# A graph-attention stack: the adjacency mask built beside the first batch, and one clock for all batches

## The chip, the cores and the metric

The kernel runs on one core of a Trainium2 chip. The metric is the device time of one execution in microseconds (us). The core has a matrix engine (TensorE; in profiles PE, its weight loads PEld), VectorE (DVE), ScalarE (ACT), GpSimd (POOL) and a queue for transfers (SP). Each engine takes its instructions from a queue of its own, and semaphores tie the queues together.

## The reference, cut to what matters

x has 32 batches of 512 nodes with 256 features; adj is one 512 x 512 matrix of integers, the same for all batches. Four layers run one after the other on each batch, each with a residual connection:

```python
h = jnp.maximum(_layernorm(x, axis=-1), 0.0)
x = x + layer(h)        # layers 0, 1, 2, 3

# inside a layer, graph attention
Wh = h @ W
e = leaky_relu((Wh @ a1)[:, :, None] + (Wh @ a2)[:, None, :])
e = where(mask, e, -inf)
out = softmax(e) @ Wh
```

Layer 0 uses the mask (adj > 0) or the diagonal. Layer 1 has another slope, layer 2 has four heads, and layer 3 has a linear layer, an attention over all nodes with no mask and 512 features, a second linear layer and a masked attention. Batches don't depend on one another.

## The kernel before, in words

The kernel has a fast path, `fast`, and a general path that runs only when a flag says that the fast path's assumptions about the data don't hold. All times here are those of the fast path.

**Arithmetic.** Exponentials of the two halves of the logit are taken per node, so that one weight of the attention is a maximum times the mask: `weights` (L335) turns a column with four transposes and makes four tiles of 128 x 512 by `max` and a product with `maskT` on VectorE (L343). `maskT` is the mask, transposed, in bfloat16; every masked layer of every batch reads it. `values` (L300) multiplies the turned activations by W and scales the result. `aggregate` (L353) multiplies weights by values. W has three more columns, products of W with the attention vectors; `finish_w` (L131) makes them with `project` (L107): transposes, a copy on ScalarE, small matmuls, and a copy on VectorE (L120). In layer 3, `sort_attend` (L527) replaces the unmasked attention by a sort: nodes are ranked by comparison scans on VectorE, scattered to DRAM in order by GpSimd's indirect transfers (L571), summed up in prefix and suffix sums (L588 to L612), and gathered back (L619). The very last batch uses `attend` (L495), which does this attention as dense matmuls.

**Order.** Four streams (`NS = 4`) take every fourth batch each. A batch is a Python generator that yields, after each piece of work, the time at which its next piece is due on a clock of the kernel's own. The loop at L722 always continues the stream with the earliest due time. A due time is made in `after_us` (L62) from what the piece spends on TensorE by a count (`spent`) and from a latency in us; a stream's own factor, `pace`, stretches both:

```python
def after_us(us):
    return begun[0] + pace[turn[0]] * (STRETCH * spent[0] / CYCLES + SLOW * us)
```

Streams start 75 clock-us apart (`LEAD`). `pace` is 1 until a stream reaches its last batch; then L713 sets it to 1.15 for batch 28, 1.025 for batch 29, 0.9 for batch 30 and 0.775 for batch 31. The clock is only a means to write instructions in an order: nothing waits for it on the chip. A fifth generator, `setup` (L213), prepares what later layers need (W1, W2, WFC, WHA, triangles for the sort); it is due at 0 and then every 4 clock-us, and draws its PSUM banks from stream 3. `bank` (L74) gives each stream two of the eight PSUM banks, by `turn`.

The order in which the program is written is a priority. The framework's scheduler builds each engine's queue from it with its own estimate of when operands are there, and may put an instruction that it thinks ready early ahead of others: in the trace, the memset of L232, written in the middle of `setup`, runs at 1.54 us. `tc.keep_in_program_order` pins an instruction behind everything that was written for its engine before it, without a wait.

**The start.** Ahead of all streams the program loads x of four batches, W0 and adj, finishes W0, and makes the mask (L190 to L202): `own` is adj > 0 on VectorE (L191), GpSimd puts ones on the diagonal (L192), sixteen transposes on TensorE and four copies on ScalarE make `maskT`. In `setup`, a reduction of adj to its least element (L218) feeds the flag.

Of the kernel before, what the change touches and what calls it, by code (L numbers as in the profile page):

```python
# [19 lines left out]
FP = mybir.dt.float32  # L20
# [4 lines left out]
OP = mybir.AluOpType  # L25
AX = mybir.AxisListType

EPS = 1.0e-5
P = 128
# [3 lines left out]
CYCLES = 2400.0  # L33
# [3 lines left out]
def fast(ctx, tc, flag, x, adj, w0, a0, w1, a1, w2, a2, mlp1_w, mlp1_b, mlp2_w, mlp2_b,  # L37
         w_fc, a_fc, w_hand, a_hand, out):
    nc = tc.nc
    B, N, F = x.shape  # L40
    NT = N // P
# [5 lines left out]
    NS = 4  # L47
    LEAD = 75.0
    SLOW = 1.5
    STRETCH = 2.0  # L50

    const = ctx.enter_context(tc.tile_pool(name="const", bufs=1))
    work = ctx.enter_context(tc.tile_pool(name="work", bufs=2))
# [3 lines left out]
    turn = [0]  # L57
    begun = [0.0]
    spent = [0.0]
    pace = [1.0] * NS  # L60

    def after_us(us):  # L62

        return begun[0] + pace[turn[0]] * (STRETCH * spent[0] / CYCLES + SLOW * us)

    def matmul(p, w, x, **flags):
        spent[0] += 4 * max(x.shape[-1], P)
        nc.tensor.matmul(p, w, x, **flags)  # L68

    def transpose(p, x, i):  # L70
        spent[0] += 2 * P
        nc.tensor.transpose(p, x, i)  # L72

    def bank():  # L74
        return psum.tile([P, N], FP, tag=f"b{turn[0]}", name="b", bufs=8 // NS)
# [3 lines left out]
    ident = const.tile([P, P], FP, name="ident")  # L79
# [23 lines left out]
    def scale_a(t, alpha):  # L103
        nc.vector.tensor_scalar_mul(t[:, :, 1:2], t[:, :, 0:1], alpha - 1.0)
        nc.vector.tensor_scalar_mul(t[:, :, 2:3], t[:, :, 2:3], 1.0 - alpha)

    def project(dst, block, k, a_cols):  # L107

        ft, n = a_cols.shape[1], a_cols.shape[2]
        p = bank()  # L110
        for f in range(ft):
            transpose(p[:, f * P:(f + 1) * P], block(k, f), ident)
        wT = work.tile([P, N], FP, tag="y", name="wT", bufs=3)
        nc.scalar.copy(wT[:, :ft * P], p[:, :ft * P])
        q = bank()
        for f in range(ft):
            matmul(
                q[:, :n], wT[:, f * P:(f + 1) * P], a_cols[:, f, :], start=(f == 0), stop=(f == ft - 1)
            )
        nc.vector.tensor_copy(dst, q[:, :n] if len(dst.shape) == 2 else q[:, :n].rearrange("p (h c) -> p h c", c=3))  # L120
# [10 lines left out]
    def finish_w(fetched, alpha):  # L131
        t, a_cols = fetched

        def block(k, f):
            c = f * P + (3 if f * P >= F else 0)
            return t[:, k, c:c + P]

        scale_a(a_cols, alpha)
        for k in range(t.shape[1]):
            project(t[:, k, F:F + 3], block, k, a_cols)  # L140
            yield
# [4 lines left out]
    adj_sb = work.tile([P, NT, N], I32, tag="w", name="adj", bufs=4)  # L146
# [10 lines left out]
    for h in range(NH):  # L157
        t, r = divmod(h * D, P)
# [27 lines left out]
    for _ in finish_w(fetched0, 0.2):  # L186
        pass


    own = work.tile([P, NT, N], FP, tag="w", name="own", bufs=4)  # L190
    nc.vector.tensor_scalar(own, adj_sb, 0.0, None, op0=OP.is_gt)  # L191
    nc.gpsimd.affine_select(  # L192
        out=own, in_=own, pattern=[[P, NT], [-1, N]], base=0, channel_multiplier=1,
        compare_op=OP.not_equal, fill=1.0,
    )
    maskT = const.tile([P, NT, N], BF, name="maskT")
    for j in range(NT):
        turn[0] = j % NS
        p = bank()
        for t in range(NT):  # L200
            transpose(p[:, t * P:(t + 1) * P], own[:, t, j * P:(j + 1) * P], ident)
        nc.scalar.copy(maskT[:, j, :], p)  # L202

    before = const.tile([P, P], FP, name="before")
    after = const.tile([P, P], FP, name="after")
    band = const.tile([P, 2 * N - P], BF, name="band")
    differ = const.tile([P, 2], FP, name="differ")
# [4 lines left out]

    def setup():  # L213

        yield from finish_w(fetched1, 0.01)


        nc.vector.tensor_reduce(differ[:, 0:1], adj_sb, AX.XY, OP.min)  # L218
        nc.vector.tensor_scalar(differ[:, 0:1], differ[:, 0:1], 0.0, None, op0=OP.is_lt)
        least = small([1], "rden")  # L220
        nc.vector.tensor_reduce(least, diag, AX.X, OP.min)
        nc.vector.tensor_scalar(differ[:, 1:2], least, 0.0, None, op0=OP.is_le)
        nc.vector.tensor_copy(W2[:, :, :, :D], raw2.rearrange("p k (h d) -> p k h d", d=D))
        nc.vector.tensor_scalar_mul(A2v[:, :, 1:2], A2v[:, :, 0:1], -0.8)
        nc.vector.tensor_scalar_mul(A2v[:, :, 2:3], A2v[:, :, 2:3], 0.8)
        for k in range(KF):
            project(W2[:, k, :, D:], lambda k, f: raw2[:, k, f * P:(f + 1) * P], k, A2)
            yield
        yield from finish_w(fetched3, 0.2)

        for tri, sign in ((before, 1), (after, -1)):
            nc.vector.memset(tri, 1.0)  # L232
            nc.gpsimd.affine_select(
                out=tri, in_=tri, pattern=[[sign, P]], base=0, channel_multiplier=-sign,
                compare_op=OP.is_gt, fill=0.0,
            )
        ties = work.tile([P, 2 * N - P], FP, tag="w", name="ties", bufs=4)
        nc.vector.memset(ties, TINY)
        nc.gpsimd.affine_select(
            out=ties, in_=ties, pattern=[[-1, 2 * N - P]], base=N - P, channel_multiplier=1,  # L240
            compare_op=OP.is_gt, fill=0.0,
        )
        nc.vector.tensor_copy(band, ties)
        yield
        yield from finish_w(fetched4, 0.2)
# [3 lines left out]
    def small(shape, name):  # L249
        return work.tile([P] + shape, FP, tag=name, name=name, bufs=2 * NS)  # L250
# [25 lines left out]
    def turn_pair(xn, hT, t0):  # L276
        p = bank()
        for k in range(KF):
            for i in range(2):
                c = (k * 2 + i) * P  # L280
                transpose(p[:, c:c + P], xn[:, t0 + i, k * P:(k + 1) * P], ident)
        nc.scalar.activation(hT[:, :, t0 * P:(t0 + 2) * P], p.rearrange("p (k n) -> p k n", k=KF), AF.Relu)  # L282

    def turned(xn, when):

        hT = work.tile([P, KF, N], FP, tag="hT", name="hT", bufs=3)
        turn_pair(xn, hT, 0)
        yield when
        turn_pair(xn, hT, 2)
        yield after_us(0.6)  # L290
        return hT
# [8 lines left out]
    def values(hT, w, rs=None):  # L300

        v = work.tile([P, NT, F + 3], FP, tag="v", name="v", bufs=4)
        for t in range(NT):
            ps = bank()
            for k in range(KF):
                matmul(
                    ps[:, :F + 3], hT[:, k, t * P:(t + 1) * P], w[:, k, :], start=(k == 0), stop=(k == KF - 1)
                )
            pj = v[:, t, F:F + 1]
            if rs is None:  # L310
                nc.scalar.activation(v[:, t, F:], ps[:, F:F + 3], AF.Exp)  # L311
                nc.scalar.activation(v[:, t, :F], ps[:, :F], AF.Copy, scale=pj)
            else:
                nc.scalar.activation(v[:, t, F:], ps[:, F:F + 3], AF.Exp, scale=rs[:, t:t + 1])
                nc.vector.tensor_scalar(  # L315
                    v[:, t, :F], ps[:, :F], rs[:, t:t + 1], pj, op0=OP.mult, op1=OP.mult
                )
            if t + 1 < NT:
                yield after_us(0)
        yield after_us(0.8)  # L320
        return v
# [372 lines left out]
    def batch(b):  # L694
        xt = xts.pop(b)
        xn, rs = new_xn(), small([NT], "rs")
        for t0 in range(0, NT, 2):
            norm(xt, xn, rs, t0, False)
        yield after_us(4)
        when = after_us(2)  # L700
        for layer in (layer0, layer1, layer2):
            xn, rs, when = yield from layer(xt, xn, rs, when)
        if b + NS < B:
            xts[b + NS] = load_x(b + NS)
        yield from layer3(xt, xn, when, b)
# [2 lines left out]

    def stream(first):
        for b in range(first, B, NS):  # L710

            if b >= B - NS:
                pace[first] = 1.15 - (NS - B + b) / (2 * NS)  # L713
            yield from batch(b)

    ready = {i: i * LEAD for i in range(NS)}
    streams = [stream(i) for i in range(NS)]
    early = setup()  # L720
    ready[NS] = 0.0
    while ready:  # L722
        i = min(ready, key=ready.get)
        if i == NS:
# [20 lines left out]
    p = bank()  # L745
# [401 lines left out]
@with_exitstack  # L1147
def kernel(ctx: ExitStack, tc: tile.TileContext, *args):
    nc = tc.nc
    keep = ctx.enter_context(tc.tile_pool(name="keep", bufs=1))  # L1150
    flag = keep.tile([1, 1], I32, name="flag")
    fast(tc, flag, *args)
    bad = nc.values_load(flag[0:1, 0:1], min_val=0, max_val=1)
    with tc.If(bad > 0):
        general(tc, *args)
# [27 lines left out]
```

## Time and profile before

| | |
|---|---|
| time, median of 3 runs | 3026.18 us (3023.26 to 3026.87) |
| span of the profiled execution | 3030.3 us |
| VectorE busy | 2269.9 us, 75% |
| ScalarE busy | 1489.6 us, 49% |
| GpSimd busy | 470.2 us, 16% |
| transfers | 245.46 MB, mean 81 GB/s |

In the page, "busy" is the time in which an engine executes; a group's line has the source line, the engine, the operation, what it writes and reads, and how often. Most matmuls are recorded by one helper, so they carry line L68, and all transposes line L72; there the names of the tiles tell what is what (`b<-W,hT` is `values`, `b<-v,w` an aggregate, `b<-ident,xn` the turning of a batch's normalised input). A matmul on float32 appears as two instructions. The timeline view lists start, duration, engine, line and tiles, and in brackets how long the engine stood idle before and what ended that.

### The profile page before, as it was taken

How to read it: one execution, taken by the hardware profiler on the slowest of the kernel's cores; microseconds unless marked ns; L12 is line 12 of the kernel's file. 1: busy time of each engine (PE TensorE's matmuls, PEld its weight loads, DVE VectorE, ACT ScalarE, POOL GpSimd, SP SyncE). 2: the span in 40 equal slices, each digit the busy share in tenths (PEclk: the TensorE clock that was granted, in tenths of full speed). 3: DMA queues.
4: the chain of work that ended last, by engine and by line, in shares of the span. 5: the costliest groups of instructions: out<-in, count | busy, mean ns of one | idle time of the engine just before them, and what ended most of it. 6: DMA issues, size and time to landing. Idle time of an engine off the chain costs nothing. (4 is left out here: it accounts for less than half of the span.)

```text
span 3030.3 us, 43501 instructions
## 1 busy us (share of the span) xinstructions
PE 2924.8 (97%) x15529; PEld 2368.3 (78%) x15529; DVE 2269.9 (75%) x5674; ACT 1489.6 (49%) x3758; POOL 470.2 (16%) x509
## 2 busy tenths in 40 slices
PE   7999999999999999999999999999999999999897
PEld 5787887877788877788877788877888877788665
DVE  4588778777877777777778777877877877767664
ACT  3444455554455554455554455554455554454445
POOL 0011111101111201112111111101111111111111
PEclk8999999999999999999999999999999999999999
DMA  3022223222223222223232223222223222212220
GB/s 91 1 88 87 75 74 102 83 90 88 74 74 102 84 89 83 80 74 102 78 95 82 81 74 102 83 90 91 71 74 102 89 84 87 74 52 82 84 97 29
DMA packets 178685, 245.46 MB, mean 81 GB/s; under 512 B 15328, under 2 KB 153886, under 8 KB 178464
## 3 DMA queue, kind: packets, MB, share of 16 engines
q1 hardware_dynamic: 148704, 144.32, 14.9%
q0 software_dynamic: 29760, 98.30, 9.8%
q8 instruction: 125, 2.05, 0.3%
q14 instruction: 96, 0.79, 0.1%
HBM read 127.46 MB, written 115.12 MB: 80 GB/s over the span
## 5 line engine op out<-in xcount | busy, mean ns | idle before, releaser
L68 PE MATMUL b<-v,w 128*128 128x257 f32 (+1 forms) x7232 | 1225.5, 322 | 22.0 <-DVE w L343 8.6
L68 PEld LDWEIGHTS b<-v,w 128*128 128x128 f32 x7232 | 1054.2, 192 | 186.7 <-issue 51.7
L343 DVE SCALAR_TENSOR_TENSOR w<-b,v,maskT 128x512 f32<-128x512 f32 x896 | 635.7, 743 | 13.3 <-PE b L72 10.5
L68 PE MATMUL b<-WFC,oT 128*128 128x256 f32 (+1 forms) x2048 | 491.5, 380 | 0.8 <-ACT v L311 0.5
L68 PEld LDWEIGHTS b<-WFC,oT 128*128 128x128 f32 x2048 | 373.6, 189 | 50.8 <-issue 1.0
L68 PE MATMUL b<-W,hT 128*128 128x259 f32 (+1 forms) x1536 | 389.1, 391 | 9.8 <-DVE v L315 8.6
L68 PEld LDWEIGHTS b<-W,hT 128*128 128x128 f32 x1536 | 282.8, 192 | 60.2 <-DVE v L315 11.0
L571 POOL DMA_INDIRECT order<-v,at x248 | 251.1, 1013 | 462.7 <-DVE seen L298 139.9
L68 PE MATMUL b<-hT,WM 128*128 128x512 f32 x512 | 251.9, 598 | 8.2 <-ACT hT L282 7.8
L359 DVE RECIPROCAL rden<-b 128x1 f32<-128x1 f32 (+1 forms) x516 | 80.2, 163 | 233.6 <-PE b L68 230.6
L677 POOL TENSOR_TENSOR x<-x,y 128x512 f32<-128x512 f32 x64 | 81.2, 1269 | 1077.3 <-ACT y L675 980.8
L619 POOL DMA_INDIRECT g<-table,at x124 | 122.5, 988 | 790.8 <-ACT y L639 287.1
L68 PE MATMUL b<-oT,WM 128*128 128x512 f32 x512 | 232.8, 597 | 0.0
L261 DVE BATCH_NORM_STATS2 st<-x 128x6 f32<-128x256 f32 x512 | 193.2, 409 | 5.6 <-DMA x<-in_x_dram 2.7
L331 ACT ACTIVATE oT<-b,bias 128x512 f32<-128x512 f32 x128 | 87.5, 686 | 216.6 <-PE b L68 216.4
L384 DVE TENSOR_TENSOR y<-q,y 128x512 f32<-128x512 f32 x192 | 132.5, 691 | 67.1 <-ACT q L383 48.2
L72 PEld LDWEIGHTS b<-ident,xn 128*128 128x128 f32 x1024 | 125.9, 142 | 69.9 <-DVE xn L272 23.6
L493 ACT ACTIVATE v<-b,ends 128x256 f32<-128x256 f32 x256 | 120.3, 470 | 122.2 <-PE b L68 115.6
L72 PE MATMUL b<-ident,xn 128*128 128x128 f32 x1024 | 159.7, 278 | 20.4 <-DVE xn L272 8.7
L282 ACT ACTIVATE hT<-b 128x512 f32<-128x512 f32 x256 | 150.2, 593 | 40.7 <-PE b L72 39.6
L68 PEld LDWEIGHTS b<-oT,WM 128*128 128x128 f32 x512 | 95.3, 191 | 93.5 <-issue 91.4
L638 ACT ACTIVATE q<-g,rden 128x512 f32<-128x512 f32 x124 | 89.5, 722 | 145.9 <-DVE rden L359 142.7
(139 smaller groups left out, 3735.0 us busy)
## 6 DMA issues: line engine op xcount, KB each, us to landing
table<-sums SPq DMA_DIRECT2D x62, 1032.0 KB
sums<-order SPq DMA_DIRECT2D x62, 516.0 KB
x<-in_x_dram SPq DMA_DIRECT2D x32, 512.0 KB
out_dram<-x SPq DMA_DIRECT2D x64, 256.0 KB
sums<-order SPq DMA_DIRECT2D x62, 129.0 KB
order<-v,at POOLq DMA_INDIRECT x248, 2.5
g<-table,at POOLq DMA_INDIRECT x124, 4.5
adj<-in_adj_dram SPq DMA_DIRECT2D x1, 1024.0 KB
```

What stands on the lines that cost most here:

```text
L68: nc.tensor.matmul(p, w, x, **flags)
L72: nc.tensor.transpose(p, x, i)
L261: nc.vector.bn_stats(st[:, i, :], xt[:, t0 + i, :])
L282: nc.scalar.activation(hT[:, :, t0 * P:(t0 + 2) * P], p.rearrange("p (k n) -> p k n", k=KF), AF.Relu)
L331: nc.scalar.activation(o[:, f, :], p, AF.Relu, bias=bias[:, f:f + 1])
L343: nc.vector.scalar_tensor_tensor(wt[:, j, :], r, t_col(j), maskT[:, j, :], op0=OP.max, op1=OP.mult)
L384: nc.vector.tensor_tensor(r, q, r, op=OP.add)
L493: nc.scalar.activation(halves[c][:, t, :F], ps[:, :F], AF.Copy, scale=ends[:, t, 0:1])
L571: nc.gpsimd.indirect_dma_start(out=orders[c], out_offset=bass.IndirectOffsetOnAxis(ap=at[:, 0, t:t + 1], axis=0), in_=halves[c][:, t, :], ...
L619: nc.gpsimd.indirect_dma_start(out=g, out_offset=None, in_=table, in_offset=bass.IndirectOffsetOnAxis(ap=at[:, 1, t:t + 1], axis=0),)
L638: nc.scalar.activation(q, z, AF.Exp, scale=rd)
L677: nc.gpsimd.tensor_tensor(xr, xr, y, op=OP.add)
```

## The change

Two things change. The mask moves from ahead of the streams into the first step of `setup`, which is now due at 7.5 on the kernel's clock, after the first pieces of batch 0; its banks come from streams 3, 2 and 1, so that those of stream 0 stay free. Its first transpose is pinned in TensorE's queue, and the reduction of adj in VectorE's. This is for letting batch 0 start beside the mask. And `pace` goes: the last four batches run on the same clock as all others.

```diff
-    pace = [1.0] * NS
 
     def after_us(us):
 
-        return begun[0] + pace[turn[0]] * (STRETCH * spent[0] / CYCLES + SLOW * us)
+        return begun[0] + STRETCH * spent[0] / CYCLES + SLOW * us
...
-    def transpose(p, x, i):
+    def transpose(p, x, i, tied=False):
         spent[0] += 2 * P
-        nc.tensor.transpose(p, x, i)
+        instruction = nc.tensor.transpose(p, x, i)
+        if tied:
+            tc.keep_in_program_order(instruction)
...
-    own = work.tile([P, NT, N], FP, tag="w", name="own", bufs=4)
-    nc.vector.tensor_scalar(own, adj_sb, 0.0, None, op0=OP.is_gt)
-    nc.gpsimd.affine_select(
-        out=own, in_=own, pattern=[[P, NT], [-1, N]], base=0, channel_multiplier=1,
-        compare_op=OP.not_equal, fill=1.0,
-    )
     maskT = const.tile([P, NT, N], BF, name="maskT")
-    for j in range(NT):
-        turn[0] = j % NS
-        p = bank()
-        for t in range(NT):
-            transpose(p[:, t * P:(t + 1) * P], own[:, t, j * P:(j + 1) * P], ident)
-        nc.scalar.copy(maskT[:, j, :], p)
-
...
     def setup():
 
+        own = work.tile([P, NT, N], FP, tag="w", name="own", bufs=4)
+        nc.vector.tensor_scalar(own, adj_sb, 0.0, None, op0=OP.is_gt)
+        nc.gpsimd.affine_select(
+            out=own, in_=own, pattern=[[P, NT], [-1, N]], base=0, channel_multiplier=1,
+            compare_op=OP.not_equal, fill=1.0,
+        )
+        for j in range(NT):
+            turn[0] = NS - 1 - j % (NS - 1)
+            p = bank()
+            for t in range(NT):
+                transpose(p[:, t * P:(t + 1) * P], own[:, t, j * P:(j + 1) * P], ident, j + t == 0)
+            nc.scalar.copy(maskT[:, j, :], p)
+        turn[0] = NS - 1
+        yield
         yield from finish_w(fetched1, 0.01)
 
 
-        nc.vector.tensor_reduce(differ[:, 0:1], adj_sb, AX.XY, OP.min)
+        tc.keep_in_program_order(nc.vector.tensor_reduce(differ[:, 0:1], adj_sb, AX.XY, OP.min))
...
     def stream(first):
         for b in range(first, B, NS):
-
-            if b >= B - NS:
-                pace[first] = 1.15 - (NS - B + b) / (2 * NS)
             yield from batch(b)
...
-    ready[NS] = 0.0
+    ready[NS] = 7.5
```

## The prediction

> **What bounds the kernel now.** I read the page's busy table first, then the span in stretches of 300 us, then the timeline of the first 25 us, and at the end the same windows view cut at the places where batches end, the waits of TensorE there, and GpSimd's timeline for those ends.
>
> ```profile
> PE 2924.8 (97%) x15529; PEld 2368.3 (78%) x15529; DVE 2269.9 (75%) x5674; ACT 1489.6 (49%) x3758; POOL 470.2 (16%) x509
> ```
>
> TensorE is busy 97% of the span: only its idle time, and the time at a low clock, can be won. Where is the idle time? The windows view has the stretch, then busy us of PE, PEld, DVE, ACT, POOL, and the granted clock:
>
> ```profile
> 0.00:300.00 300.00, 272.20 (x1438) 220.97 (x1439) 199.48 (x541) 122.48 (x323) 29.17 (x38) 0.96 0.21 66
> 1200.00:1500.00 300.00, 295.39 (x1603) 242.71 (x1601) 232.50 (x580) 157.38 (x403) 48.54 (x54) 1.00 0.27 87
> 2700.00:3031.00 331.00, 294.51 (x1436) 225.83 (x1434) 200.62 (x474) 151.03 (x353) 51.19 (x53) 0.96 0.21 69
> ```
>
> The middle loses 4.6 us in 300 (1.5%), the first 300 us lose 27.8 and the last 331 lose 36.5. The change touches just these two ends. Timeline of the start:
>
> ```profile
> 10.08 1.23 DVE L191 TENSOR_SCALAR own<-adj 128x2048 f32<-128x2048 int32 x1 [2.22 <-DMA adj<-in_adj_dram]
> 11.22 0.15 DVE L120 COPY W<-b 128x3 f32<-128x3 f32 x1
> 11.29 2.28 DVE L218 TENSOR_REDUCE differ<-adj 128x1 f32<-128x2048 int32 x1
> 11.38 1.92 POOL L192 TENSOR_SCALAR_AFFINE_SELECT own<-own 128x2048 f32<-128x2048 f32 x1 [9.06 <-DVE W L120]
> 13.35 3.54 PE L72 MATMUL b<-ident,own 128*128 128x128 f32 x16 [3.11 <-POOL own L192]
> 13.49 0.15 DVE L120 COPY W<-b 128x3 f32<-128x3 f32 x1
> 16.72 0.71 PE L72 MATMUL b<-ident,xn 128*128 128x128 f32 x5
> 18.06 1.14 PE L68 MATMUL b<-W,hT 128*128 128x259 f32 x4
> 23.69 0.75 DVE L343 SCALAR_TENSOR_TENSOR w<-b,v,maskT 128x512 f32<-128x512 f32 x1 [0.22 <-PE b L72]
> ```
>
> TensorE stands 3.11 us before the mask's transposes, and batch 0, whose xn has been ready since 7.86 (the last of the three L272 rows: 6.81 + 1.05), queues behind them to 16.6. W0's last three columns come at 13.64, behind the 2.28 us reduction of adj.
>
> At the end, GpSimd's last additions (two per batch) show when batches 27 to 31 end: 2759, 2929, 2979, 3014, 3024.
>
> ```profile
> 2757.34 1.26 POOL L677 TENSOR_TENSOR x<-x,y 128x512 f32<-128x512 f32 x1 [7.85 <-ACT ends L492]
> ...
> 2927.90 1.27 POOL L677 TENSOR_TENSOR x<-x,y 128x512 f32<-128x512 f32 x1 [10.51 <-ACT y L675]
> ```
>
> Batch 0 ends at 298 (its L677 rows begin at 288.60 and 296.27), so 27 batches took 2461 us, 91.15 each; batch 28 takes 170. The windows between those ends:
>
> ```profile
> 2759.00:2850.00 91.00, 79.58 (x418) 62.97 (x417) 69.96 (x166) 36.27 (x90) 12.33 (x14) 0.94 0.30 100
> 2850.00:2929.00 79.00, 71.67 (x346) 52.04 (x345) 49.09 (x109) 34.89 (x75) 15.08 (x16) 0.96 0.27 88
> 2929.00:3031.00 102.00, 84.65 (x379) 64.32 (x377) 42.61 (x91) 49.22 (x110) 11.75 (x12) 0.96 0.12 40
> ```
>
> Idle 11.4, 7.3 and 17.4, together 36.1 us; TensorE's work left at 2759 is 235.9 us. The hole in the first window, in tens of us:
>
> ```profile
> 2820.00:2830.00 10.00, 7.29 (x36) 5.56 (x34) 9.52 (x25) 3.66 (x8) 0.26 (x1) 1.00 0.29 89
> 2830.00:2840.00 10.00, 4.56 (x17) 3.28 (x18) 8.25 (x22) 4.04 (x10) 0.00 (x0) 0.63 0.22 72
> ```
>
> VectorE is 95% busy where TensorE starves, and what TensorE waits for between 2800 and 2850 are links of norm and sort:
>
> ```profile
> PE b L72 <- ACT rs L264: 3.4, 2, 2.4
> PE b L68 <- DVE tot L593: 3.0, 1, 3.0
> ```
>
> **What the Trainium skill says.** "TensorE: Matmul & The Clock Gate", section "What's actually happening": the array runs at half clock until about 3.4 us of sustained work, and falls back after an idle window. The trace agrees: the mask's 16 transposes take 3.54 us (221 ns each, after the idle start), eight later ones 0.87 us (109 ns); and the clock reads 0.63 in the hole above. So a hole costs more than its idle time. Same page, "Architectural detail: the array is 16× 32×32, not 1× 128×128": VectorE's and ScalarE's queues are strictly first in, first out, and only weight loads are pulled ahead on TensorE. The trace agrees: batch 0's ready transposes stay behind the mask's.
>
> **The change, part by part.**
>
> Start. The same operations stay (one conversion 1.23, one select 1.92, 16 transposes, four casts of 0.6, one reduction 2.28); only their places move. The mask cannot be earlier: adj lands at 10.08, so the select still ends at 13.3. New: (a) batch 0's first four transposes are pinned ahead of the mask's, the second four may be too; they fit into TensorE's present wait. (b) The reduction is pinned behind what VectorE has been given, so W0's second copy can follow the first at about 11.4. Then values may begin near 11.6 instead of 18.06. TensorE's wait shrinks from 3.11 us to the 1.4 from 10.24 (end of the W0 projections) to 11.6: 1.7 us won. (c) W1, W2, WFC and WHA get clock times 11.5 later than before (first step 7.5 + 4 against 0), so they fill batch 0's stalls instead of going ahead of it. Batch 0's values (16 matmul instructions, 1.14 for four: 4 us warm, up to 8 cold) and the mask's transposes (1.8 warm, 3.5 cold) after 11.6 end between 18 and 20, so the weights at L343 start about 4 us ahead of 23.69. The moved reduction has behind it batch 0's reciprocals, which wait for an aggregate of eight matmul instructions (1.9 us) anyway, so its 2.28 is nearly hidden. Bounds: 1.7 (only idle removed) to 5 (the whole lead of batch 0 kept, since its work to about 100 us is a chain: TensorE is idle 21 of the first 100 us). I take 3.
>
> End. No instruction is added or removed. By the formula in after_us a batch has 301 clock-us (264 for batch 31, which attends without sort). Batches 28 to 31 start at 2106.7, 2181.7, 2256.7 and 2331.7 on that clock. With factors 1.15, 1.025, 0.9 and 0.775 they end at 2453, 2490, 2528 and 2536; with 1 at 2408, 2483, 2558 and 2596. So before, all four end close together, but batch 28's gathers (clock 2366) fall on batch 29's sort (2365): VectorE's scans, sums and norms coincide, which is the hole at 2800 to 2850. After, stages stay a quarter of a batch apart as in the middle of the run, and the streams drain one by one.
> My sum for the 235.9 us of work after 2759: batch 28 now ends 91 us later at the middle's 1.6%: 1.5 us idle. Three streams left: as between 200 and 300 us at the start, which lost 1.0 of 100: 1 us. Two left: as between 100 and 200, which lost 5.7: 5. Batch 31 alone: the 17.4 of the last window already hold the lone chain at the end (13.7 of them in the last 31 us); I add nothing for the hurried batches 29 to 31 there and 0.6 for a longer lone stretch: 18. Together 25.5 against 36.1: 10.6 won. Low clock: in the holes about 1.7 + 1.4 (2830 to 2850) + 2.9 (clock 0.86 in 2900 to 2925) = 6.0 us of busy time were lost; the new two-stream stretch loses 7% of some 45 us, 3. Net 3, so the end gives 13 or 14, I take 13. Unknown: the lone stretch, from 14 to 40 us idle.
>
> 3026 - 3 - 13 = 3010.
>
> **The rivals.**
> Slower: the drain with fewer streams is worse than the holes it removes. For it: batch 31 ends 38 clock-us behind batch 30 instead of 9, and the first 60 us, with one stream, lost 17.1. If two streams idle 10% of 85 (8.5), the lone stretch 30% of 60 (18) and the end 14, with 4 ahead, that is 44.5, 8 more than now; with 4 lost to the low clock and 2 won at the start, 3036. Against it: batch 31 attends, which is dense TensorE work (64 aggregate and 64 projection instructions of about 0.24 us).
> No change: the holes come from the order of an engine's queue against real DMA times, not from the factors, and reappear; only the start counts: 3023.
> Better: VectorE never saturates, batch 31 runs under batch 30 throughout, and the small hole of 2610 to 2650 (4.5 us idle, when batch 28 was already slowed) goes as well: end 27, start 3: 2996.
> A variant of mine: the second half of batch 0's transposes and its values are queued behind the mask's; then the start gives 0 and the time is 3013.
>
> **How the numbers follow.** Mine with its variant 0.43 (3002 to 3019), better 0.20, no change 0.17, slower 0.20. Same means within 6 us of 3026, 3020 to 3032. Faster: 0.43 + 0.20 + 0.03 of the no-change case = 0.66; same: 0.14 + 0.01 from the milder end of slower = 0.15; slower 0.19. The range goes from just under the better case to the slower one: 2992 to 3036.
>
> **What would show it.** Right: values (L312) of batch 0 start before 15 us and L343 near 19; GpSimd's additions of batch 28 end near 2850, of batches 29 to 31 some 90, 75 and 30 apart; TensorE idles under 28 us after 2759 and VectorE is nowhere over 95% in that stretch. Wrong: L343 still near 23; a new TensorE wait on the mask in front of the values; idle over 36 us after batch 27, most of it after batch 30's end.

## The result and the profile after

The changed kernel takes 3002.16 us (median of 4 runs, 2999.36 to 3004.19) against 3025.83 us: ratio 0.9922, 95% interval 0.9905 to 0.9940, or 24 us less. On the chip of the last experiments the ratio was 0.9904 (0.9888 to 0.9919).

The busy table of the page, and the windows at the start, in the middle and at the end (stretch; busy us of PE, PEld, DVE, ACT, POOL; granted clock; transfers):

```profile
PE 2910.2 (97%) x15529; PEld 2364.7 (79%) x15529; DVE 2266.7 (76%) x5674; ACT 1487.5 (50%) x3758; POOL 468.7 (16%) x509
```

```profile
0.00:300.00 300.00, 273.40 (x1458) 222.73 (x1459) 200.72 (x545) 126.43 (x333) 29.95 (x39) 0.97 0.22 68
...
1200.00:1500.00 300.00, 295.42 (x1606) 242.83 (x1605) 233.32 (x581) 157.10 (x400) 48.19 (x53) 1.00 0.25 84
...
2700.00:2998.00 298.00, 273.54 (x1343) 212.41 (x1341) 189.06 (x447) 139.22 (x333) 41.22 (x43) 0.96 0.21 68
```

TensorE executes the same 15529 instructions and is busy 14.6 us less. The mean granted clock rose from 0.990 to 0.994; by an estimate from these two figures (0.4% of 2925 us) that is about 12 of the 14.6. The middle is as it was. In the first 300 us it does 20 instructions more with 1.2 us less idle.

GpSimd's last additions again mark the ends of batches (two rows to a batch, of which the second is shown). Timeline of GpSimd in the changed kernel, batches 28, 29, 30 and 31:

```profile
2829.66 1.27 POOL L679 TENSOR_TENSOR x<-x,y 128x512 f32<-128x512 f32 x1 [3.46 <-ACT y L677]
...
2908.34 1.27 POOL L679 TENSOR_TENSOR x<-x,y 128x512 f32<-128x512 f32 x1
...
2970.66 1.27 POOL L679 TENSOR_TENSOR x<-x,y 128x512 f32<-128x512 f32 x1 [7.10 <-ACT y L677]
...
2990.37 1.26 POOL L679 TENSOR_TENSOR x<-x,y 128x512 f32<-128x512 f32 x1 [4.24 <-ACT y L677]
```

The start of the last addition of a batch shows where the time went:

| batch | before | after | earlier by |
|---|---|---|---|
| 0 | 296.27 | 292.27 | 4.0 |
| 24 | 2474.13 | 2466.88 | 7.3 |
| 27 | 2757.34 | 2742.55 | 14.8 |
| 28 | 2927.90 | 2829.66 | 98.2 |
| span | 3030.3 | 2997.6 | 32.7 |

(The two profiled executions lie further apart than the medians: 32.7 us against 24.) So 4 to 7 us come from the start, 7.5 from the time between the ends of batches 24 and 27, when batch 28 already ran with its factor before, and 17.9 after batch 27. In that last part TensorE's idle time fell from 35.6 to 23.1 us, for nearly the same work (1148 instructions before, 1138 after), and its busy time by 5.5. Batch 28 now follows batch 27 by one regular step. The windows from the end of batch 27 to that of batch 28, from there to the end of the span, and the second of these cut at the ends of batches 29 and 30:

```profile
2742.55:2829.66 87.11, 85.88 (x463) 69.55 (x462) 67.51 (x166) 43.82 (x112) 14.93 (x16) 1.00 0.25 82
2829.66:2997.60 167.94, 146.07 (x675) 109.44 (x673) 89.08 (x196) 75.03 (x168) 22.87 (x24) 0.94 0.17 58
...
2829.66:2908.34 78.68, 73.19 (x369) 56.86 (x368) 53.38 (x120) 34.70 (x81) 14.44 (x17) 0.93 0.24 80
2908.34:2970.66 62.32, 59.26 (x249) 43.08 (x247) 27.75 (x56) 31.27 (x67) 4.63 (x5) 0.97 0.12 41
2970.66:2997.60 26.94, 13.62 (x60) 9.50 (x59) 7.96 (x20) 9.05 (x21) 3.79 (x3) 0.85 0.10 33
```

Only 1.2 us are idle between the ends of batches 27 and 28, against 18.9 of 170.56 before. Timeline of the start:

```profile
10.71 1.23 DVE L204 TENSOR_SCALAR own<-adj 128x2048 f32<-128x2048 int32 x1 [2.75 <-DMA adj<-in_adj_dram]
11.85 0.22 DVE L121 COPY W<-b 128x3 f32<-128x3 f32 x2
12.06 1.97 PE L71 MATMUL b<-ident,xn 128*128 128x128 f32 x8 [1.68 <-DVE W L121]
13.86 1.23 PE L67 MATMUL b<-W,hT 128*128 128x259 f32 x2
14.89 2.80 PE L71 MATMUL b<-ident,own 128*128 128x128 f32 x16
17.52 0.60 PE L67 MATMUL b<-W,hT 128*128 128x259 f32 x2
22.72 2.28 DVE L220 TENSOR_REDUCE differ<-adj 128x1 f32<-128x2048 int32 x1
24.91 2.72 DVE L345 SCALAR_TENSOR_TENSOR w<-b,v,maskT 128x512 f32<-128x512 f32 x4
33.66 0.15 DVE L361 RECIPROCAL rden<-b 128x1 f32<-128x1 f32 x1
```

Batch 0's transposes and the first of its values now run ahead of the mask's transposes. Yet its weights (L345) begin at 24.91, later than the 23.69 of before: the reduction of adj stands in front of them. (0.63 us of the difference is no doing of the kernel: adj arrived later in this execution, and its conversion on VectorE began at 10.71 instead of 10.08.) What came earlier is the next link, batch 0's first reciprocal, at 33.66. In the kernel before it stood behind copies for WFC that setup had put ahead of it:

```profile
38.19 0.16 DVE L120 COPY WFC<-b 128x3 f32<-128x3 f32 x1 [2.56 <-PE b L68]
...
38.47 0.22 DVE L359 RECIPROCAL rden<-b 128x1 f32<-128x1 f32 x2
```

### The profile page after: what moved, and what is told of

The parts are those of the page before. It is cut to its first block, busy times and chain, and to the rows that moved or that the text cites. A ratio compares the mean times of both kernels' runs of the same rounds, so it can differ in the third digit from the quotient of the medians.

```text
span 2997.6 us, 43508 instructions
## 1 busy us (share of the span) xinstructions
PE 2910.2 (97%) x15529; PEld 2364.7 (79%) x15529; DVE 2266.7 (76%) x5674; ACT 1487.5 (50%) x3758; POOL 468.7 (16%) x509
## 4 chain that ended last, share of the span: by engine, by line
PE 80%; DVE 12%; ACT 4%; issue 2%; DMA 1%; SPq 0%; POOL 0%; POOLq 0%; DVEq 0%; ACTq 0%
PE b L67 73%; PE b L71 8%; DVE w L345 2%; DVE st L263 2%; DVE xn L274 1%; DVE junk L552 1%; DVE y L386 1%; DMA order<-v,at 1%; DVE v L317 1%; DVE y L676 1%; DVE x L418 1%; ACT hT L284 0%; DVE xn L270 0%; DVE g L636 0%; ACT y L677 0%
## 5 line engine op out<-in xcount | busy, mean ns | idle before, releaser
L67 PE MATMUL b<-v,w 128*128 128x65 f32 (+1 forms) x7232 | 1221.4, 321 | 19.4 <-DVE w L345 12.4
L345 DVE SCALAR_TENSOR_TENSOR w<-b,v,maskT 128x512 f32<-128x512 f32 x896 | 636.3, 741 | 5.1 <-PE b L71 1.9
L67 PEld LDWEIGHTS b<-W,hT 128*128 128x128 f32 x1536 | 282.7, 192 | 58.5 <-DVE v L317 11.2
L71 PEld LDWEIGHTS b<-ident,xn 128*128 128x128 f32 x1024 | 127.3, 142 | 60.3 <-DVE xn L274 17.9
L67 PEld LDWEIGHTS b<-oT,WM 128*128 128x128 f32 x512 | 95.5, 192 | 94.6 <-issue 92.9
```

Of the source, the lines that this page charges most:

```text
L71: instruction = nc.tensor.transpose(p, x, i)
L345: nc.vector.scalar_tensor_tensor(wt[:, j, :], r, t_col(j), maskT[:, j, :], op0=OP.max, op1=OP.mult)
```

## The experiments

All ratios are to the kernel before on the same chip. For the end I also use the time from batch 24's last addition to the end of the profiled span, which leaves the start out: 556.2 us before, 530.7 changed.

**Each part alone.**

```diff
 changed kernel: the factors put back
+            if b >= B - NS:
+                pace[first] = 1.15 - (NS - B + b) / (2 * NS)
```

> The changed kernel with the factors 1.15, 1.025, 0.9, 0.775 put back: the mask's move alone. In the trace of the changed kernel batch 0 ends 4.0 us earlier than before and batch 24 7.3 us earlier, ahead of anything that the factors touch. Theory A (the two parts add up; the start is worth what batch 24 shows): 3018 to 3022. Rival (the lead of the start is lost again in the drain, where streams wait for one another): 3024 to 3027.

Measured: 0.9982 (0.9976 to 0.9989), 5.5 us; from batch 24 on 557.4 us. The start's lead survives to the end.

```diff
 kernel before: the factors taken out
-            if b >= B - NS:
-                pace[first] = 1.15 - (NS - B + b) / (2 * NS)
```

> The kernel before with the factors taken out and nothing else: the end alone. Theory A: 24 us less the start's 4 to 7, so 3006 to 3010, with TensorE idle about 24 us after batch 27 instead of 36 and no window where VectorE is above 95% and TensorE below 75%. Rival (the holes come from the queues' order against real transfer times, not from the factors): holes of 10 us remain, 3018 or more.

Measured: 0.9922 (0.9910 to 0.9935), 24 us; from batch 24 on 533.1. The parts add up: 0.9982 x 0.9922 = 0.9904, as the changed kernel had on the last chip; the 0.9922 of the first chip has an interval of 0.9905 to 0.9940. The clock is worth about four times the mask.

**Which factors.** The changed kernel with `pace[first]` set from a tuple:

```diff
+                pace[first] = (1.15, 1.025, 1.0, 1.0)[first]     # slow two
+                pace[first] = (1.0, 1.0, 0.9, 0.775)[first]      # fast two
+                pace[first] = 1.15                               # all slow
```

> The changed kernel with factors 1.15, 1.025, 1, 1: only the slowing. Batch 28's gather (clock 2366) falls on batch 29's sort (2365) as before, all else is spread. Theory A (lined up stages make the hole): a hole of about 10 us between the ends of batches 27 and 28, 3012 to 3018. Rival B (hurrying batches 30 and 31 did the harm): 3000 to 3005.

> The changed kernel with factors 1, 1, 0.9, 0.775: only the hurrying. Batch 28's gather (2333) is 28 clock-us ahead of batch 29's sort (2361), as in the changed kernel; batch 29's gather (2408) is 10 ahead of batch 30's sort (2418). Theory A: no hole before batch 28's end, a small one after, and the last two batches end closer together: 3000 to 3008. Rival B: 3012 to 3020.

> The changed kernel with the factor 1.15 for all of the last four batches: as far from 1 as the largest of before, but the four keep their distances (batch 28's gather at clock 2366, batch 29's sort at 2388). Theory A (what costs is that the stages of neighbours fall together): no hole, 3000 to 3006. Rival (a batch slowed against the ones before it costs in itself, as batch 28 was from its start): 3010 or more.

Measured: slow two 0.9952 (0.9937 to 0.9966), fast two 0.9925 (0.9913 to 0.9937), all slow 1.0016 (1.0009 to 1.0022); from batch 24 on 541.6, 536.6 and 567.9 us. Slow two has the forecast idle time (11.4 us between the ends of batches 27 and 28). Slowing cost more than hurrying, as I had it: against the changed kernel 11 and 6 us from batch 24 on, where the kernel before, with all four factors, lost 25.5, so in these single profiles more than their sum. But all slow, which should have been harmless, is the worst, and its time is where the rival of its forecast, that a slowed batch costs in itself, had it. It has several holes; this is the largest, in the windows view and in the waits of TensorE in it:

```profile
2880.00:2900.00 20.00, 8.65 (x58) 7.04 (x56) 10.89 (x27) 7.03 (x12) 6.38 (x6) 0.67 0.43 146
```

```profile
PE b L68 <- DVE tot L596: 6.6, 1, 6.6
PE b L72 <- DVE y L387: 4.6, 2, 3.1
```

VectorE is busy only 10.89 of 20 us there, so it isn't full. TensorE waits for one link of the prefix sums (`tot`) and for gathered rows on their way through the nonlinearity (`y`). The timeline of VectorE and TensorE shows what held `tot`:

```profile
2895.71 0.76 DVE L637 SCALAR_TENSOR_TENSOR g<-g,ends 128x516 f32<-128x516 f32 x1 [4.88 <-DMA g<-table,at]
...
2898.05 0.42 DVE L596 TENSOR_TENSOR tot<-sums 128x258 f32<-128x258 f32 x1
...
2898.62 1.20 PE L68 MATMUL b<-tot,before 128*128 128x258 f32 x2 [6.55 <-DVE tot L596]
```

VectorE itself stood 4.88 us for a gathered row that hadn't landed, with the other batch's sums behind that instruction. After batch 24, such waits of VectorE for a gather add up to 12.4 us in all slow, against 2.6 in the changed kernel and 1.3 before; so this is a loss of all slow's own, which the kernel before doesn't have.

In the changed kernel there is the opposite, VectorE 98% busy beside a TensorE that never starves, and once, after batch 27, 100%:

```profile
2575.00:2600.00 25.00, 24.97 (x168) 22.22 (x167) 24.63 (x57) 12.93 (x29) 6.58 (x7) 1.00 0.14 49
...
2760.00:2770.00 10.00, 9.98 (x70) 8.99 (x68) 10.00 (x21) 3.70 (x10) 4.00 (x5) 1.00 0.12 43
```

So a full VectorE need not make a hole, and a hole needs no full VectorE. What the kernels with holes share is seen in GpSimd's timeline. By start times, the first of the next batch's eight scatters (L571 before) against a batch's fourth gather (L619):

| kernel | 28 and 29: gather, scatter | 29 and 30: gather, scatter | us from batch 24 |
|---|---|---|---|
| changed | 2753, 2764 | 2842, 2852 | 530.7 |
| clock alone | 2763, 2774 | 2852, 2862 | 533.1 |
| fast two | 2762, 2777 | 2872, 2857 | 536.6 |
| slow two | 2810, 2777 | 2859, 2864 | 541.6 |
| before | 2819, 2792 | 2902, 2873 | 556.2 |
| all slow | 2800, 2785 | 2889, 2874 | 567.9 |

Wherever a scatter begins before the fourth gather of the batch ahead, the two stages meet: gathered rows of one batch go through VectorE, ScalarE and TensorE while the other batch scatters and sums. In this table: no meeting, 531 to 533 us; one, 537 to 542; two, 556 or more. The steps are not sharp: five more profiles without a meeting, from the runs below, took 530.5 to 534.9 us, so fast two is hardly apart from them, and the one meeting made by hand below took 549.5.

**A meeting made by hand.** To part the meeting from the factors, I delayed batch 28 alone, once before its gathers and once behind them:

```diff
 late gathers
-        yield after_us(9)
+        yield after_us(9) + (33.0 if b == B - NS else 0.0)
         got, when, gs = [], [], []
 late after
         mlp_in(oT, got[-1], NT - 1)
-        yield after_us(1.0)
+        yield after_us(1.0) + (33.0 if b == B - NS else 0.0)
```

> The changed kernel, all batches on one clock, with batch 28's gathers 33 clock-us later and all that follows in batch 28 with them; batch 29's eight scatters then stand between them. Theory G: a hole where TensorE idles 5 us or more at the scatters, 8 to 14 us slower than the changed kernel of this job. Rival (such a meeting is harmless, the factors cost in other ways): within 3 us of it.

> The control to the late gathers: the same 33 clock-us, in the same batch, but put behind its gathers; gathers and scatters stay apart. Theory G: within 3 us of the changed kernel of this job. Rival (holding batch 28 back costs in itself): as slow as with the late gathers.

> The changed kernel once more, on the chip of these runs: 0.9905 to 0.9925 of before. If it comes out above the two kernels without or with an early reduction (0.9895 and 0.9902), the reduction's place in front of batch 0's first weights costs about 2 to 5 us; if at 0.990, nothing.

Measured: late gathers 0.9962 (0.9949 to 0.9976), late after 0.9894 (0.9879 to 0.9910), changed again 0.9904 (0.9888 to 0.9919). The same delay costs 17 us where it makes the stages meet (3018.70 against 3001.53; 8 to 14 were forecast) and nothing where it doesn't (2998.82). From the end of batch 27 to that of batch 28, late gathers first, late after second:

```profile
2739.06:2882.64 143.58, 128.09 (x668) 102.28 (x668) 95.74 (x231) 65.45 (x156) 25.02 (x29) 0.94 0.23 74
```

```profile
2741.74:2865.51 123.77, 120.58 (x666) 99.19 (x665) 95.49 (x231) 64.26 (x156) 24.63 (x28) 0.99 0.27 86
```

The work is equal (668 and 666 matmul instructions, VectorE 95.7 and 95.5); idle 15.5 against 3.2, and 7.5 us more busy time at a clock of 0.94 against 0.99. GpSimd with late gathers shows the third and fourth gather after the scatters; the first two were placed early in the queue all the same and start at 2727 and 2729, where changed again has 2730 and 2732:

```profile
2728.65 0.96 POOL L621 DMA_INDIRECT g<-table,at  x1 [0.30 <-issue]
...
2759.93 1.03 POOL L573 DMA_INDIRECT order<-v,at  x1 [16.10 <-DVE at L556]
...
2770.91 0.97 POOL L573 DMA_INDIRECT order<-v,at  x1 [0.81 <-DMA order<-v,at]
2787.37 0.98 POOL L621 DMA_INDIRECT g<-table,at  x1 [15.49 <-DVE q L384]
2799.00 0.96 POOL L621 DMA_INDIRECT g<-table,at  x1 [10.65 <-ACT y L641]
```

The last two don't wait for GpSimd, which had been idle 15.49 and 10.65 us; they wait for VectorE and ScalarE to be done with a buffer of gathered rows, of which there are two.

**Is it GpSimd's queue?** The factors kept, but the order on GpSimd as in the changed kernel:

```diff
 mask's move alone, factors in
             yield sort
+            while b in (B - 3, B - 2) and turned_in.get(b - 1, 0) < NT:
+                yield begun[0] + 1.0
...
+                if b in (B - 3, B - 2):      # scatter queued behind gathers[b - 1]
+                    tc.add_manual_dep(scatter.ins, gathers[b - 1].ins.name, ...)
```

> The mask moved and the factors 1.15, 1.025, 0.9, 0.775 kept, but batch 29's scatters are queued on GpSimd behind batch 28's last gather, and batch 30's behind batch 29's. Theory G (with the factors the eight scatters of one batch stand between the gathers of the batch before, and that makes the holes): most of the factors' loss of 25 us comes back, 12 to 22 us less than the mask's move alone with its ratio of 0.9982, so 0.991 to 0.994 of before; four gathers take 20 to 28 us instead of 34 and 50. Rival V (VectorE's load, or the uneven speeds themselves): 0.997 or more.

Measured: 0.9985 (0.9978 to 0.9992), the same as the mask's move alone; from batch 24 on 561.0. Theory G falls, and the ratio lies where rival V had it. The fourth gather (2816 and 2897) is now before the first scatter (2818 and 2898), but the four gathers still take 35 us for batch 28 (22 for batch 29), and a hole comes with the scatters that follow at once; again VectorE is half idle in it:

```profile
2900.00:2920.00 20.00, 9.39 (x25) 4.64 (x24) 10.45 (x19) 6.49 (x12) 8.18 (x8) 0.66 0.46 146
```

The hold moves batch 29's scatters from 2789 to 2818, so it may also have cost what it saved: at 2828 VectorE begins a wait of 7.54 us for scattered rows to come back. More buffers for gathered rows would have been the cleaner test and weren't tried.

**The parts of the start.** Three changes to the changed kernel:

```diff
 no reduction
-        tc.keep_in_program_order(nc.vector.tensor_reduce(differ[:, 0:1], adj_sb, AX.XY, OP.min))
-        nc.vector.tensor_scalar(differ[:, 0:1], differ[:, 0:1], 0.0, None, op0=OP.is_lt)
+        nc.vector.memset(differ[:, 0:1], 0.0)
 early reduction: these two lines moved up
         turn[0] = NS - 1
         yield
+        tc.keep_in_program_order(nc.vector.tensor_reduce(...)); nc.vector.tensor_scalar(...)
         yield from finish_w(fetched1, 0.01)
 due at 0
-    ready[NS] = 7.5
+    ready[NS] = 0.0
```

> The changed kernel without the reduction of adj to its least element (2.28 us on VectorE); the flag's first column is set to zero instead, so the test for negative entries of adj is left out. In the changed kernel's trace the reduction stands right before batch 0's first weights: they start at 24.91, though their operands are there at about 22.9. Theory A (batch 0's chain sets the start): batch 0 and all after it 2 us earlier, 2999.5 to 3001. Rival (setup's projections fill TensorE there anyway): 3001.5 to 3003.

> The changed kernel with the reduction moved up right behind the mask's conversion, into VectorE's idle stretch of 12 to 16 us; it then stands ahead of W0's second copy again, as in the kernel before. Theory A: values are held by about 2 us at 14.3, the weights lose their wait; the sum is about nothing, 3001 to 3003. Rival (the values wait for the mask's transposes anyway): 2999.5 to 3001.

> The changed kernel with setup due at 0 instead of 7.5: the mask is in setup, but it and all later steps of setup keep their early place. Theory A (the start's gain is that the projections of W1, W2 and WFC no longer stand ahead of batch 0's reciprocals and of its first values): most of the 4 us of the start goes, 3005 to 3008. Rival (the gain is the mask's place alone): 3001 to 3003.

Measured: 0.9895 (0.9880 to 0.9910), 0.9902 (0.9886 to 0.9917) and 0.9916 (0.9902 to 0.9929); the changed kernel had 0.9904 and 0.9922 on two chips. None of the three is told apart from it by time, so by time the place of the reduction costs nothing that can be told; and the 3003.12 us of "due at 0" are near its rival's forecast and not in that of theory A. The traces say more: without the reduction batch 0's weights begin at 23.18, with the early one at 22.85, and batch 0's last addition starts at 287.1 and 286.4; due at 0 they begin at 22.25, and batch 0 still ends late, at 295.6, where the kernel before had 296.3. In nine profiles of kernels with the changed start that differ only later this number lay between 287.7 and 293.7. Part of that spread is the arrival of adj: its conversion on VectorE begins anywhere from 9.37 to 11.52 us in the fourteen profiles. Counted from there, batch 0's last addition starts after 278.4 to 282.7 us in those nine, and after 286.0 us due at 0, 286.2 before and 286.9 with the clock alone, the three in which setup is due at 0; after 276.8 without and 276.2 with the early reduction. Due at 0 also has a copy for WFC right in front of the first reciprocal again, as before:

```profile
9.60 1.23 DVE L204 TENSOR_SCALAR own<-adj 128x2048 f32<-128x2048 int32 x1 [1.71 <-DMA adj<-in_adj_dram]
...
34.32 0.16 DVE L121 COPY WFC<-b 128x3 f32<-128x3 f32 x1 [2.06 <-PE b L67]
...
34.60 0.22 DVE L361 RECIPROCAL rden<-b 128x1 f32<-128x1 f32 x2
```

Up to the end of batch 0, then, as far as one profile of "due at 0" can show it, the lead comes from setup's later place and not from the mask's place. That this lead makes the 5.5 us of the whole run is not shown: the times don't tell "due at 0" apart, and at the end of batch 24, counted the same way, it stands where the mask's move alone stands (2461.2 us both).

## Why the prediction was right, and where it was off

**Direction and size.** I forecast 3010, faster, 2992 to 3036; it became 3002. Both parts help and they add up, as I had it; both were sized too small, 16 us together where the result has 24.

**Start: 3 us forecast, 5.5 measured** (3.3 to 7.3 by the interval). The path was wrong in two steps, so what is right in the size is luck. Values were to begin near 11.6 and end by 20; they began at 13.86, because the eight transposes of xn did not fill TensorE's wait: they started only at 12.06, after the copies of W0, and took 1.97 us. Of the values, all but the first two instructions stayed behind the mask's transposes, as in my variant. The weights were to lead by 4 us and the moved reduction to be "nearly hidden"; it stands right in front of the weights, which came 1.2 us later than before (0.6 when counted from the conversion of adj). L343 "still near 23" was one of my signs of being wrong, and it showed. The lead at the end of batch 0 came from part (c), setup standing back: first reciprocal 4.8 us earlier, and no lead left in "due at 0".

**End: 13 us forecast, 24 measured.** The step "batch 28's gathers fall on batch 29's sort" held, and the hand-made meeting shows that one such meeting can cost 17 us. TensorE's idle time after batch 27 was to fall to 25.5 us and fell to 23.1; that sum is near partly by luck, since its terms with four batches left, three, two and one came to 1.2, 5.5, 3.1 and 13.3 us where I had 1.5, 1, 5 and 18. The mis-sized term is the time before batch 27's end: I gave nothing for it, having put the hole of 2610 to 2650 into the better case, and it was worth 7.5 us (275.7 us between the ends of batches 24 and 27 instead of 283.2; 276.1 with the clock alone). Slowing batch 28 is not by itself the reason: all slow has the same factor for it and took 276.0. The others came out near: idle gave 12.4 instead of 10.6; busy time 5.5 instead of 3, of which the ten instructions fewer are about 2 (at the 0.2 us that one takes here, 231.95 / 1138). The drain was cheap, as I had it: lone batch 31 idles 13.3 us after batch 30's last addition starts, where before the last 17.3 us idled 12.6.

**The reason inside the hole** does not hold: I read VectorE's 95% as the limit. In the lines that I had shown, VectorE was at 8.25 of 10 us where TensorE starved most (2830 to 2840). Holes exist with VectorE at half load, and where it was 98% and 100% busy in the changed kernel TensorE lost 0.03 and 0.02 us. What a hole shows is a chain of short links (gather, multiply, exponential, transposes; sums and their matmuls) for which TensorE waits in the order of its queue. The no-change rival had it that holes come from a queue's order against real DMA times and stay when the factors go. Such a wait is in all slow's hole, but the rival is wrong on the change: without the factors the holes between the ends of batches 27 and 28 went (1.2 us idle). A smaller slip of the forecast: eight later transposes take 1.03 us in the trace before (at 212.88) when they are counted like the mask's 3.54; its 0.87 is eight times the 109 ns from one start to the next.

**Open:** how the factors cost their 24 us. That they do is shown by the clock alone, and that a meeting can cost 17 us is shown by the two delays; that the factors cost by way of the meetings is likely, but not shown. All slow loses more than before with meetings half as deep, in part by VectorE's waits for gathers, and the held scatters lose without any overlap in start times. A rival therefore stands: batches whose pieces are spread unevenly against each other lose in themselves, meeting or not. Late after shows only that one single hold behind the gathers is harmless. Which queue hands the delay on in the kernel before is open too; GpSimd's order alone is not it. VectorE's load is not it in all slow and the held scatters; in the holes of the kernel before and of late gathers VectorE was 83% to 95% busy, so a part of it there is not ruled out.

The rival "slower" was wrong by its drain: with two streams left, between the ends of batches 29 and 30, TensorE idled 3.1 of 62.3 us, not 10%.

## What to carry to other kernels

When several independent streams share in-order queues, their distance is a resource: it is worth keeping stages made of short dependent links (sort, scatter, gather) of two streams apart, also in the drain, and checking it by the start times of one marker instruction of each. Squeezing the last streams so that they end together may cost more than the thin tail would have; here it cost 24 us. Holes are also paid in clock: late gathers has 12.3 us more idle time than late after, and 7.5 us more busy time for nearly the same instructions.

## What the runs showed that I had not expected

VectorE can be 98% busy (24.63 of 25 us) while TensorE is at 24.97 of 25. Kernels that differ only after batch 0 had its end anywhere from 287.7 to 293.7 us, with the clock granted between 25 and 50 us from 0.75 to 0.87: a trace of the start shows an effect of 4 us only if it is repeated, or counted from the arrival of the data that the start waits for.
